# Two half-image stores become one whole-image store, and the load of x is written one stage later

## Chip, cores and metric

The kernel runs on one core of a Trainium2 chip. The metric is the device time of one execution in microseconds (us). Before the change three runs took 1347.35, 1353.44 and 1364.31 us, so the median is 1353.44 us. A comparison of two kernels of this kind can tell about 2% from no change.

## The reference

The input `x` is 32 images of 256 channels by 32 x 32 pixels, in float32. Two layers are applied one after the other, each on a group norm of its input, and each added to its input:

```
x = x + conv3x3_quantised(group_norm(x), weight, bias)      # 256 -> 256 channels, values rounded to fp16's grid
x = x + involution7x7(group_norm(x))                        # 16 groups of 16 channels
```

The convolution rounds its inputs, weights and products to a 5-bit-exponent, 10-bit-mantissa float. The involution computes a 7 x 7 kernel for every pixel and group from the pixel itself:

```
y = relu(w1 @ x * scale + shift)             # 64 channels
w = w2 @ y + b2                              # 16 groups * 49 taps, for each pixel
out[g, c, h, w] = sum over 49 taps of w[g, tap, h, w] * x[g, c, h+i, w+j]
```

## The kernel before

One image is a tile `x` of 128 partitions x 2 halves of channels x 1024 pixels in float32: 8192 B a partition, 1 MB in all. The pool `xpool` has five such tiles, so the tile of image b is used again by image b + 5. An image goes through these steps:

- `load_x` (L106) loads the tile with two DMAs of 512 KB, in runs of 4096 B, from the queue of SyncE (SP).
- `front` does both group norms on ScalarE and VectorE, the 3 x 3 convolution on TensorE (the matmuls of L332), the residual, `w1` (L377) and the transposition of pixels to partitions (L396).
- `weights` (L411) multiplies by `w2`; VectorE evicts the result into `w_sb` (L435).
- `scatter` (L476) writes `w_sb` to a buffer `wd` in DRAM, seven DMAs of 160 KB for each band of 8 image rows (`k` = 0 to 3), in runs of 640 B, from SP's queue. They come in two parts: four DMAs, and three a stage later.
- `load_bands` (L497) reads `wd` back in a skewed form, 16 DMAs a band: two from SP's queue, 14 from GpSimd's (POOL). There are three band buffers, so a band's load waits until the band three places before it has been used.
- `sums` (L522) contracts the bands with the pixels on TensorE, and `add_windows` (L538) adds the result into the image's tile on VectorE.
- `store` (L543) writes a half of the image (512 pixels of every channel, 512 KB in runs of 2048 B) to the output, from SP's queue.

The order of the work is written out by hand. A loop runs over stages n; an image takes 16 stages (`per = 2 * M` with M = 8), and each step has a lag that says at which stage it is written down. Every engine then carries out its own instructions in that order and waits where data is not there. SyncE does nothing but issue DMAs, in order: one that must wait holds up all that stand behind it. In terms of the stage within an image's turn of `sums` (modulo 16), SP's queue holds:

```
stage  3: 4 scatters (k=0), 2 band loads     stage  4: 3 scatters (k=0)
stage  7: 4 scatters (k=1), 2 band loads     stage  8: 3 scatters (k=1)
stage 11: 4 scatters (k=2), 2 band loads     stage 12: store of the first half, 3 scatters (k=2)
stage 13: 4 scatters (k=3)                   stage 14: 3 scatters (k=3)
stage 15: store of the second half, 2 band loads
stage 17: 2 loads of x, for the image five places later, into the tile that was just stored
```

That is 40 DMAs an image. The scatters belong to the next image or the one after it, since `weights` runs 18 stages ahead. SP's DMAs take their completion semaphores from a ring of eight: an SP DMA waits until the one eight places before it has landed. The load of x waits as well until the store of the tile's former image has landed.

The second half's store is written down right after the image's last `add_windows`, which is the last to write the tile. The load's stage comes from `LOAD = -63`: image b is loaded at stage 16 b - 63, which is stage 17 of image b - 5. `front` starts on it at 16 b - 56.

Of the kernel before, what the change touches and what calls it, by code (L numbers as in the profile page):

```python
# [14 lines left out]
B, C, H, W = 32, 256, 32, 32  # L15
N = H * W
NT = 512
# [23 lines left out]
SIDES = 2  # L41
JC = W // SIDES
K = H // TR
M = K * SIDES
# [26 lines left out]
EARLY = CH + 4 + CH * CR  # L71
LATE = K1 * SW + 2 * 2 * SW
FRONT = -56
LOAD = -63
LEAD = 18


# [1 line left out]
def tile_quant_conv_then_involution(  # L79
# [23 lines left out]
    def load_x(b):  # L103
        xt = xpool.tile([P, CH, N], F32, tag="x", name=f"x_{b}")
        for h in range(CH):
            nc.sync.dma_start(xt[:, h], x[b, h * P : (h + 1) * P])  # L106
        return xt
# [85 lines left out]
    def quantize_weights(kh):  # L193

        nc.vector.tensor_scalar(wq[:, kh], staged[kh], F16_MAX, -F16_MAX, ALU.min, ALU.max)
        nc.gpsimd.memset(bands[kh], 0.0)
        if kh == CH - 1:
            nc.gpsimd.memset(w_sb, 0.0)
# [204 lines left out]
    def weights(b, r0):  # L403

        pws = [ps_w.tile([P, 2, 2, SW], F32, tag=f"pw{i}", name=f"pw{i}") for i in range(2)]
        for r in range(2):
            for t in range(T):
                for i in range(2):
                    half = slice(i * CR, (i + 1) * CR)
                    dj = slice(2 * t, min(2 * t + 2, K1))  # L410
                    nc.tensor.matmul(  # L411
                        pws[i][t * TW : (t + 1) * TW, : dj.stop - dj.start, r],
                        y_sb[b % 2][half, (r0 // 2 + r) * W : (r0 // 2 + r + 1) * W],
                        w2_sb[half, dj],
                        start=True,
                        stop=True,
                    )
        for i in range(2):
            for e in range(2):
                p = P if e == 0 else (K1 // 2) * TW  # L420
                for r, rows, d0, d1, at in ring_pieces(b, r0 + 2 * i):
                    evict(pws[i][:p, e, r : r + rows], e, r, rows, d0, d1, at)
# [42 lines left out]
    def scatter(b, k, part):  # L465

        at = (b * H + k * TR) % RING
        for dj in range(part, K1, 2):
            t, e = divmod(dj, 2)
            to = bass.AP(  # L470
                tensor=wd.tensor,
                offset=wd.offset + k * TR * ROW + dj * WPIX + (K1 - 1 - dj) * WB,
                ap=[[WPIX, TW], [ROW, TR], [1, WB]],
            )
            rows = w_sb[t * TW : (t + 1) * TW, e, at : at + TR]
            nc.sync.dma_start(to, rows.rearrange("p s a r v -> p s (a r v)"))  # L476

    def load_bands(b, k):

        band = bands[(b * K + k) % NBAND]  # L480
        side = WINC * WB + PAD
        for i, j in enumerate(ORDER):
            cut = max(0, PAD1 - j)
            n = (K1 - cut) * WB + PAD
            src = bass.AP(
                tensor=wd.tensor,
                offset=wd.offset + k * TR * ROW + (j + PAD1) * WPIX + cut * WB,
                ap=[[ROW - V, TR], [(W - 1 - 2 * j) * WPIX - cut * WB, SIDES], [1, n]],
            )
            to = band[j::JC]  # L490
            to = bass.AP(
                tensor=to.tensor,
                offset=to.offset + (j + cut) * WB,
                ap=[to.ap[0], [side + (JC - 1 - 2 * j - cut) * WB, SIDES], [1, n]],
            )
            queue = nc.sync if j in BY_SYNC else nc.gpsimd
            queue.dma_start(to, src)  # L497
# [10 lines left out]
    def sums(b, m):  # L508

        k, d = divmod(m, SIDES)  # L510
        j0 = 0 if d else PAD1
        band = bands[(b * K + k) % NBAND][:, d]
        px = pixels[(b * K + k) % NPIX][:, d]
        for h in range(CH):
            for v in range(2):
                for g, at, top, f, l in windows(b, m):
                    p = slice(g * KP, (g + 1) * KP)
                    of = band[p, V * g * XR + j0 * WB : V * g * XR + (j0 + WINI) * WB]
                    of = of.rearrange("p (j a r v) -> p j a r v", a=A, r=WIN, v=V)
                    for t in range(T):  # L520
                        a = h * T + t
                        nc.tensor.matmul(  # L522
                            at[t * TW : (t + 1) * TW, h, :, f - top : l - top],
                            px[p, a, v * GC : v * GC + TW],
                            of[:, :, a, f - top : l - top, v],
                            start=(h, v) == (0, 0),
                            stop=(h, v) == (CH - 1, 1),
                        )

    def add_windows(b, m):  # L530

        d = m % SIDES
        to = x_tiles[b].rearrange("p h (r c) -> p h r c", c=W)
        j0 = d * (JC - PAD1)
        for g, at, top, f, l in windows(b, m):
            x_at = to[:, :, f:l, j0 : j0 + WINI]
            of = at.rearrange("p h j r -> p h r j")[:, :, f - top : l - top]
            nc.vector.tensor_tensor(x_at, of, x_at, ALU.add)  # L538

    def store(b, k):  # L540

        cols = slice(k * NT, (k + 1) * NT)
        nc.sync.dma_start(out[b].rearrange("(h p) n -> p h n", p=P)[:, :, cols], x_tiles[b][:, :, cols])  # L543


# [3 lines left out]
    def due(n, lag):  # L549

        b, i = divmod(n - lag, per)
        return (b, i) if 0 <= b < B else (None, None)

    with tc.manual_schedule():
        fronts = {}
        for n in range(FRONT, B * per + 2):
            b, i = due(n, FRONT)
            if i == 0:
                fronts[b] = front(b)
            later = list(fronts)  # L560
            for part in range(2):
                for b in list(later):
                    got = next(fronts[b], fronts)
                    if got is fronts:
                        fronts.pop(b)
                    if got is not LATER:
                        later.remove(b)
            if n in (FRONT + CH, FRONT + CH + 4):
                quantize_weights((n - FRONT - CH) // 4)
            b, i = due(n, 0)  # L570
            if b is not None and i % 2 == 0:
                sums(b, i // 2)
            b, i = due(n, 1)
            if b is not None and i % 2 == 0:
                add_windows(b, i // 2)
                if i // 2 == M - 1:
                    store(b, 1)
                    x_tiles.pop(b)

            b, i = due(n, 2)  # L580
            if b is not None and i == 2 * (M - 1 - SIDES):
                store(b, 0)
            b, i = due(n, -LEAD)
            if b is not None and i % 2 == 0:
                weights(b, i // 2 * WR)

            for part in range(2):
                b, i = due(n, -LEAD + 1 + part)
                if b is not None and i % 2 == 0:
                    for k in range(K):  # L590
                        if i // 2 == min((k + 1) * TR // WR, H // WR - 1):
                            scatter(b, k, part)
            b, i = due(n, LOAD)
            if i == 0 and b > 1:
                x_tiles[b] = load_x(b)

            b, i = due(n, 3 - 4 * NBAND)
            if b is not None and i % 4 == 0:
                load_bands(b, i // 4)
# [38 lines left out]
```

## Time and profile before

| | before |
|---|---|
| median of 3 runs | 1353.44 us |
| the profiled execution | 1344.24 us |
| its span in the profile | 1342.5 us |
| TensorE matmul, busy | 1253.6 us, 93% |
| VectorE, busy | 818.8 us, 61% |
| ScalarE, busy | 733.3 us, 55% |
| GpSimd, busy | 1014.4 us, 76% |
| moved by DMA | 361.85 MB, 270 GB/s on the mean |

Busy time is the time in which an engine has an instruction in work. SyncE has no row of its own: its instructions only issue DMAs. Sixteen DMA engines carry all queues' transfers; q1 is the queue of SP, and q0 that of GpSimd. A packet is one contiguous run of bytes that a DMA engine moves. In a list of waits, a row names the waiting engine and line, then what ended the wait, then the microseconds in total, how often, and the longest.

### The profile page before, as it was taken

What the parts mean: (1) busy time and instruction counts of PE and PEld (TensorE: products, weight loads), DVE (VectorE), ACT (ScalarE), POOL (GpSimd) and SP (SyncE); (2) the same over time, 40 slices, a digit from 0 to 9 for tenths busy, and PEclk for the clock granted to TensorE, in tenths of its full rate; (3) what the DMA queues carried; (4) which work ended last, traced back from release to release, by engine and by line L of the source; (5) the groups of instructions that cost most, each with busy time, mean ns of one, the idle gap of its engine ahead of it and who ended that gap; (6) DMA issues with size and microseconds to landing.
All of it is one profiled execution on the core that took longest, in us unless ns stands there. A gap on an engine that the chain in (4) does not pass through costs nothing.

```text
span 1342.5 us, 65799 instructions
## 1 busy us (share of the span) xinstructions
PE 1253.6 (93%) x27648; PEld 763.7 (57%) x27648; DVE 818.8 (61%) x2539; ACT 733.3 (55%) x1731; POOL 1014.4 (76%) x1818
## 2 busy tenths in 40 slices
PE   5899999999999999999999999999999999999665
PEld 2356566565555655556655556666555566556454
DVE  3466666565666665656665666766666666666442
ACT  5775656455656556556545655655556564553300
POOL 9067878777787778777778787788777877788785
PEclk9999999999999999999999999999999999999987
DMA  6089999999999999999999999999999999999995
GB/s 228 11 237 295 271 293 293 279 266 281 272 286 282 291 285 270 283 263 280 293 282 283 270 288 282 293 297 296 281 288 275 277 284 290 271 281 266 278 274 166
DMA packets 360724, 361.85 MB, mean 270 GB/s; under 512 B 75056, under 2 KB 304752, under 8 KB 359152
## 3 DMA queue, kind: packets, MB, share of 16 engines
q1 hardware_dynamic: 278512, 229.38, 56.8%
q0 software_dynamic: 81920, 128.28, 33.9%
q8 instruction: 220, 3.60, 1.1%
q14 instruction: 72, 0.59, 0.1%
HBM read 176.60 MB, written 180.76 MB: 266 GB/s over the span
## 4 chain that ended last, share of the span: by engine, by line
PE 60%; DMA 23%; POOL 7%; issue 3%; ACT 3%; DVE 2%; SPq 1%; POOLq 0%; DVEq 0%; ACTq 0%
PE pc L332 25%; PE acc L522 19%; DMA band<-wd 17%; PE pw L411 11%; POOL band L497 7%; DMA wd<-w_sb 6%; PE pt L396 3%; PE py L377 3%; ACT junk L214 1%; SPq L476 1%; DVE w_sb L435 1%; DMA x<-in_x 1%; ACT xn L273 0%; SPq L497 0%; ACT xq L273 0%
## 5 line engine op out<-in xcount | busy, mean ns | idle before, releaser
L497 POOL DMA_DIRECT2D band<-wd x1792 | 980.3, 549 | 315.7 <-DMA band<-wd 182.0
L435 DVE TENSOR_TENSOR w_sb<-pw,late_sb 128x224 f32<-128x224 f32 (+7 forms) x1280 | 330.4, 322 | 419.5 <-PE pw L411 419.2
L332 PE MATMUL pc<-xq,wq 128*128 128x496 f16 (+3 forms) x2304 | 535.2, 379 | 20.3 <-ACT xq L273 18.3
L522 PE MATMUL acc<-band,pixels 64*32 64x190 f32 (+1 forms) x16384 | 426.6, 332 | 51.8 <-DMA band<-wd 42.7
L522 PEld LDWEIGHTS acc<-band,pixels 64*32 64x32 f32 x16384 | 304.7, 107 | 159.7 <-issue 81.1
L332 PEld LDWEIGHTS <-wq 128*128 128x128 f16 x2304 | 206.7, 98 | 316.1 <-issue 102.7
L411 PE MATMUL pw<-late_sb,y 64*32 64x224 f32 (+1 forms) x8192 | 288.9, 333 | 10.8 <-issue 9.4
L538 DVE TENSOR_TENSOR x<-acc,x 128x380 f32<-128x380 f32 (+1 forms) x512 | 262.0, 512 | 32.2 <-PE acc L522 23.2
L411 PEld LDWEIGHTS pw<-late_sb,y 64*32 64x32 f32 x8192 | 186.5, 106 | 38.1 <-issue 21.0
L400 ACT COPY pixels<-pt 128x512 f32<-128x512 f32 x128 | 73.7, 576 | 228.6 <-PE pt L396 228.6
L214 ACT ACTIVATE junk<-x 128x512 f16<-128x512 f32 (+1 forms) x192 | 146.4, 763 | 14.7 <-DVE x L348 12.2
L214 ACT ACTIVATE junk<-x,mean 128x1024 f16<-128x1024 f32 x128 | 147.1, 1149 | 4.3
L245 ACT ACTIVATE s<-back,eps 128x2 f32<-128x2 f32 x64 | 18.9, 296 | 178.6 <-DVE back L230 178.6
L346 DVE TENSOR_SCALAR q<-pc 128x512 f16<-128x512 f32 x128 | 87.2, 681 | 17.6 <-PE pc L332 17.6
L273 ACT ACTIVATE xn<-x,off,rstd 128x512 f32<-128x512 f32 x128 | 96.2, 800 | 0.0
L348 DVE SCALAR_TENSOR_TENSOR x<-q,early_sb,x 128x512 f32<-128x512 f16 x128 | 94.2, 736 | 0.3
L396 PEld LDWEIGHTS pt<-ident,xn 128*128 128x128 f32 x512 | 63.9, 142 | 26.3 <-issue 2.5
L396 PE MATMUL pt<-ident,xn 128*128 128x128 f32 x512 | 78.0, 275 | 0.1
L273 ACT ACTIVATE xq<-x,off,rstd 128x1024 f16<-128x1024 f32 x64 | 75.7, 1227 | 0.0
L235 ACT ACTIVATE mean<-back 128x2 f32<-128x2 f32 x64 | 12.6, 196 | 101.4 <-DVE back L230 101.4
L377 PE MATMUL py<-xn,early_sb 128*64 128x512 f32 x256 | 62.2, 606 | 0.9 <-ACT xn L273 0.9
L224 DVE STREAM_TRANSPOSE across<-sums 128x32 f32<-128x32 f32 x128 | 26.3, 205 | 33.6 <-ACT junk L214 32.4
(40 smaller groups left out, 369.3 us busy)
## 6 DMA issues: line engine op xcount, KB each, us to landing
wd<-w_sb SPq DMA_DIRECT2D x896, 160.0 KB
band<-wd POOLq DMA_DIRECT2D x1664, 70.5 KB, 4.6
x<-in_x SPq DMA_DIRECT2D x64, 512.0 KB
out<-x SPq DMA_DIRECT2D x64, 512.0 KB
band<-wd POOLq DMA_DIRECT2D x128, 60.5 KB, 4.6
band<-wd SPq DMA_DIRECT2D x128, 50.5 KB
band<-wd SPq DMA_DIRECT2D x128, 40.5 KB
band<-in_w SPq DMA_DIRECT2D x2, 1152.0 KB
```

The costliest lines, as they stand in the source:

```text
L214: nc.scalar.activation(junk[:, n0:n1], src[:, h, n0:n1], func, bias=bias, accum_out=self.sums[:, i : i + 1])
L273: nc.scalar.activation(dst, src, AF.Identity, bias=self.off[:, one], scale=self.rstd[:, one])
L332: nc.tensor.matmul(pc.rearrange("p (r c) -> p r c", c=W)[:, r0 - nt * RT : r1 - nt * RT, c0:c1], wq[:, kh, k, mh * P : (mh + 1) * P], xq[: ...
L346: nc.vector.tensor_scalar(q, pc, F16_MAX, -F16_MAX, ALU.min, ALU.max)
L348: nc.vector.scalar_tensor_tensor(xt[:, mh, cols], q, bias_sb[:, mh : mh + 1], xt[:, mh, cols], ALU.add, ALU.add)
L377: nc.tensor.matmul(py[i * CR : (i + 1) * CR], w1_sb[:, kh, :], px[:, :, i], start=kh == 0, stop=kh == CH - 1,)
L396: nc.tensor.transpose(pt[:, i, h * P : (h + 1) * P], xn[:, h, (m + i) * P : (m + i + 1) * P], ident)
L411: nc.tensor.matmul(pws[i][t * TW : (t + 1) * TW, : dj.stop - dj.start, r], y_sb[b % 2][half, (r0 // 2 + r) * W : (r0 // 2 + r + 1) * W], w ...
L435: nc.vector.tensor_tensor(to, of[:, :, d0:d1], bias[:, :, d0:d1], ALU.add)
L497: queue.dma_start(to, src)
L522: nc.tensor.matmul(at[t * TW : (t + 1) * TW, h, :, f - top : l - top], px[p, a, v * GC : v * GC + TW], of[:, :, a, f - top : l - top, v], ...
L538: nc.vector.tensor_tensor(x_at, of, x_at, ALU.add)
```

## The change

The store of an image is one DMA at stage 15, 1 MB in runs of 4096 B, for the first 31 images. The last image is stored in halves as before, at stages 12 and 15. The load of x is written down at stage 16 b - 62 instead of 16 b - 63.

```diff
-LOAD = -63
+LOAD = -62
...
-    def store(b, k):
+    def store(b, *halves):
 
-        cols = slice(k * NT, (k + 1) * NT)
+        cols = slice(halves[0] * NT, (halves[-1] + 1) * NT)
         nc.sync.dma_start(out[b].rearrange("(h p) n -> p h n", p=P)[:, :, cols], x_tiles[b][:, :, cols])
...
                 if i // 2 == M - 1:
-                    store(b, 1)
+                    store(b, *([1] if b == B - 1 else range(2)))
                     x_tiles.pop(b)
 
             b, i = due(n, 2)
-            if b is not None and i == 2 * (M - 1 - SIDES):
+            if b == B - 1 and i == 2 * (M - 1 - SIDES):
                 store(b, 0)
```

## The prediction

> **What bounds the kernel now.** I read the page's head and its 40 slices first, then the steady stretch from 165 to 1197 us by itself, then the waits of SP's queue in that stretch, because both edits are in that queue.
>
> ```profile
> PE 1253.6 (93%) x27648; PEld 763.7 (57%) x27648; DVE 818.8 (61%) x2539; ACT 733.3 (55%) x1731; POOL 1014.4 (76%) x1818
> DMA  6089999999999999999999999999999999999995
> ```
>
> The DMA row is 9 from the fifth slice to the last but one, and TensorE is nearly as full. The stretches table sharpens this (columns: length, then each engine's busy time, the granted clock, the DMA engines' busy share, GB/s):
>
> ```profile
> 165.00:1197.00 1032.00, 1003.57 (x22468) 610.87 (x22465) 659.84 (x2059) 594.81 (x1407) 795.15 (x1454) 1.00 0.97 283
> ```
>
> TensorE is busy 1003.57 of 1032 us and the sixteen DMA engines 0.97 of the time. Both are near full. Between the ends of successive images' last `add_windows` lie 39.66 us on the mean (28 images), 37.84 at least, 42.36 at most; the eight shortest average 38.17. The DMA engines' own work is 0.9655 x 39.66 = 38.3 us an image, so neither resource leaves much room. Waits of the same stretch:
>
> ```profile
> POOL band L497 <- DMA band<-wd: 156.5, 195, 2.9
> ...
> POOL band L497 <- DMA wd<-w_sb: 21.3, 22, 3.1
> ...
> PE acc L522 <- DMA band<-wd: 12.7, 10, 2.7
> ```
>
> GpSimd's wait for its own earlier transfers is back-pressure of full engines; its wait for scatters is 0.8 us an image; TensorE waited for a band ten times. The waits of SP's queue:
>
> ```profile
> SPq L476 <- DVE w_sb L435: 79.4, 53, 5.1
> SPq L106 <- DMA out<-x: 72.9, 26, 4.1
> SPq L476 <- DMA wd<-w_sb: 31.8, 50, 2.2
> ...
> SPq L476 <- DMA x<-in_x: 13.5, 18, 1.6
> ```
>
> The second row is the one the change touches: 26 times the load of x stood 2.8 us for the store to land, with all scatters behind it. One such place, in SP's own order:
>
> ```profile
> 649.34 0.94 SPq L543 DMA_DIRECT2D out<-x  x1
> 650.37 1.79 SPq L497 DMA_DIRECT2D band<-wd  x2
> 654.91 0.83 SPq L106 DMA_DIRECT2D x<-in_x  x2
> 656.10 3.05 SPq L476 DMA_DIRECT2D wd<-w_sb  x4
> ```
>
> SP is idle from 652.16 to 654.9; the scatters then follow without a gap, so they were ready and late.
>
> **LOAD.** Between stage 15 (store, two band loads) and stage 19 (the next scatters) SP's queue holds nothing but the two loads. Moving them from stage 17 to 18 moves them past no DMA of SP and none of POOL: both queues keep their order, and what the loads wait for is unchanged. Cost: 0, from both sides. The work that hides any later landing is `front`, which starts six stages on, about 15 us (16 stages in 39.66 us); the loads' packets end 6.65 us after issue (mean of 25 images).
>
> **The first half's store goes** (31 images). SP loses one issue of 0.504 us (median of the 64), 15.6 us in all. It stands in a stretch (8 us before the image's end to 6 us after) in which SP issues without pause: its waits there sum to about 1.5 us an image. So what follows on SP comes earlier: by 0.5 us at least, and by up to 1.9 us if the transfer's own engine time counts too (256 packets x 87 ns / 16 = 1.39 us). Room for that exists: the second store issues 3.3 us after the `add_windows` it needs (mean of 25).
>
> **Packets of 4096 B.** The trace's packet records give, in the steady stretch, 35.6 ns for the 640 B writes (median 32) and 87.1 ns for the 2048 B stores (median 84). A line through the medians is 8.4 ns + 0.0369 ns a byte, hence 160 ns for a 4096 B store; the median of the 4096 B loads is 159. One packet instead of two saves 8.4 ns; 256 pairs / 16 engines x 8.4 = 0.13 us an image, **4.2 us** over 31. The other end is the loads' mean, 213 ns, which would add 39 ns a pair: +0.62 us an image, +19 us. I take the line, because the store rows show no tail (87 against a median of 84), unlike the loads.
>
> [...]
>
> **The store lands later after its issue, from an earlier issue.** Mean of 25 images for the second half's store: first packet 2.19 us after issue, last 3.08 us later, the load 0.57 us after that, the load's first packet 1.11 us on. The new store has the same 16 packets an engine, each longer. Kept at the same share of the engines, 3.08 becomes 3.08 x 160/87 = 5.7 (+2.6 us). At the pace of the x load (32 packets an engine in 5.5 us) it is 2.8 (-0.3). With the earlier issue (-0.5 to -1.9) the load moves by something between **-2.2 and +2.1 us**. I take 0: from the first store's issue to the second's landing the engines are full (0.97 and 1.01 before 653 in the table below), and the same bytes have to pass before the load may go, wherever in that stretch they stand.
>
> The load's place also makes a dip, which does not grow with the store: q1 is empty for 0.57 + 1.11 us whatever was stored.
>
> ```profile
> 645.00:649.00 4.00, 4.00 (x106) 2.63 (x87) 2.61 (x8) 1.66 (x2) 2.16 (x5) 1.00 1.01 286
> 649.00:653.00 4.00, 4.00 (x108) 2.78 (x107) 2.09 (x7) 1.21 (x3) 3.80 (x7) 1.00 0.97 292
> 653.00:656.00 3.00, 3.00 (x98) 2.47 (x102) 2.30 (x8) 1.96 (x4) 2.51 (x5) 1.00 0.93 287
> ```
>
> [...]
>
> What a shift of the load costs: behind it stand the scatters of band 0, and GpSimd's loads of that band wait for those, 0.59 us on the mean. Their last packet lands 2.8 us before TensorE uses the band. In the images with the longest periods GpSimd didn't wait there at all, and over 25 images the load's lateness and the period don't rise together (correlation -0.27). So a shift of a few tenths is absorbed.
>
> **Sum.** LOAD 0, shift 0, packets -4.2: 1344.24 - 4.2 = 1340.0 us for the profiled execution (span 1342.5 and 1.7 around it). The median before stands 0.68% above it; so scaled, **1349 us**. SP's 0.5 us are counted inside the shift.
>
> **Rivals.**
>
> *Slower.* The landing takes the larger figure, SP's stall grows from 2.8 to nearly 5 us, the scatters of band 0 are later by up to 2.1 us, and GpSimd, which has only 0.59 us of wait to lose there, starts the band later. For it: the row of 72.9 us. Against: TensorE's lead of 2.8 us, and the work that is conserved. It decides from 1 us an image on (27 waiting loads, 27 us = 2%). At 1.4 us, two thirds of the bound: +38 - 4 = 1378, scaled **1387**; at all 2.1, +57, 1406.
>
> *Faster.* SP is what lags: everything behind the first store moves up, scatters land before GpSimd asks, and the dip is filled. The dip costs 0.66 us an image (mean shares 0.97, 0.85, 0.75, 0.77 from 7 to 11 us after the image's end), SP's issue 0.5: 27 x 1.16 + 4.2 = 36, 1308, scaled **1317**. For it: SP's unbroken issue. Against: 0.97 of DMA share, and the floor of 38.17 us an image, which allows 40 us at most.
>
> *It does not do what it says.* A 4096 B store costs what the loads cost on the mean: +19, 1363, scaled **1372**, still within 2%.
>
> **How the numbers follow.** Forecast 0.46 (own range 1338 to 1362), costlier packets 0.17, slower 0.21, faster 0.16. About 2% is what a measurement of this kernel can tell from no change; the first two lie within it, 0.63. The range runs from just inside the fast rival to the slow one's first price: 1320 to 1387, leaving out a tenth on each side.
>
> **What will show it.** 4096 B store packets near 160 ns; 8192 fewer q1 packets or slightly less; SP's wait for the store between 2 and 4 us a load; GpSimd's wait for scatters near 21 us in the stretch; the DMA share still 0.97 and the mean period 39.5 us. Wrong if that wait passes 4 us and GpSimd's wait for scatters doubles (slower), or if the period comes near 38.2 (faster).

## The result and the profile after

The changed kernel takes **1368.33 us** (median of 16 runs) where the kernel before took 1355.22 (16 runs): a ratio of **1.0101, 95% interval 1.0079 to 1.0124** (the quotient of the two medians is 1.0097). The loss is small, within 2%, and its interval leaves 1 out. The profiled execution after has a span of 1370.0 us. The one of before, 1344.24 us with a span of 1342.5, is faster than all 16 runs of before (1344.98 to 1364.31), which matters below.

The page of the changed kernel, first TensorE's row and the DMA slices, then the packets and the stretch from 165 to 1197 us:

```profile
PE 1257.5 (92%) x27648; PEld 762.3 (56%) x27648; DVE 825.9 (60%) x2539; ACT 734.0 (54%) x1731; POOL 1012.4 (74%) x1818
...
DMA  6088999999999989999999999999999999999995
...
q1 hardware_dynamic: 270080, 229.38, 55.7%
q0 software_dynamic: 81920, 128.28, 33.0%
```

```profile
165.00:1197.00 1032.00, 990.19 (x22039) 601.97 (x22038) 648.18 (x2025) 580.80 (x1373) 780.63 (x1427) 0.99 0.94 277
```

The packets of q1 are fewer and their bytes the same. But in the same 1032 us TensorE is busy 990.19 us instead of 1003.57, and the DMA engines 0.94 of the time instead of 0.97: both near-full resources have become less full. Most of that is the one fast execution of before, for a second profile of the same instructions (`halves_load62`, below) reads

```profile
165.00:1197.00 1032.00, 992.64 (x22212) 604.69 (x22219) 650.82 (x2022) 585.49 (x1382) 787.49 (x1435) 1.00 0.95 279
```

The waits of SP's queue, and one store with what follows it:

```profile
SPq L106 <- DMA out<-x: 113.3, 26, 5.8
SPq L476 <- DVE w_sb L435: 95.7, 69, 6.1
```

```profile
661.46 0.43 SPq L543 DMA_DIRECT2D out<-x  x1
661.99 2.55 SPq L497 DMA_DIRECT2D band<-wd  x2
668.94 0.83 SPq L106 DMA_DIRECT2D x<-in_x  x2
670.12 2.61 SPq L476 DMA_DIRECT2D wd<-w_sb  x4
```

SP's wait for the store grew from 72.9 to 113.3 us, 1.6 us an image. It looks like the cause. The experiments speak against it. A first hint is in the means over 25 images: the store is now issued 1.43 us after the image's last `add_windows` instead of 3.33, and the load of x goes out at 9.04 us instead of 9.17. SP waits longer because it arrives earlier; the load and the scatters behind it are where they were.

Waits of TensorE and of POOL's queue in the same stretch:

```profile
POOL band L497 <- DMA band<-wd: 175.8, 192, 3.5
...
POOL band L497 <- DMA wd<-w_sb: 25.9, 30, 2.6
...
PE pw L411 <- issue: 19.8, 15, 2.7
...
PE acc L522 <- DMA band<-wd: 9.7, 11, 2.6
PE acc L522 <- issue: 7.6, 8, 1.9
```

GpSimd waits 19 us longer for its own earlier band transfers (156.5 before), TensorE no longer than before for bands (12.7 before), and its stops that the profile can only call issue are 27 us here; on the same two lines they were 11.8 us before (8.2 and 3.6). What these are is told further down.

### The profile page after: what moved, and what is told of

Its sections match the earlier page's. It is cut to its first block, busy times and chain, and to the rows that moved or that the text cites. A ratio compares the mean times of both kernels' runs of the same rounds, so it can differ in the third digit from the quotient of the medians.

```text
span 1370.0 us, 65799 instructions
## 1 busy us (share of the span) xinstructions
PE 1257.5 (92%) x27648; PEld 762.3 (56%) x27648; DVE 825.9 (60%) x2539; ACT 734.0 (54%) x1731; POOL 1012.4 (74%) x1818
## 4 chain that ended last, share of the span: by engine, by line
PE 64%; DMA 19%; POOL 5%; issue 5%; DVE 3%; ACT 2%; SPq 2%; POOLq 0%; DVEq 0%; ACTq 0%
PE pc L332 26%; PE acc L522 20%; DMA band<-wd 14%; PE pw L411 11%; POOL band L497 5%; DMA wd<-w_sb 4%; PE py L377 3%; PE pt L396 3%; SPq L476 1%; ACT junk L214 1%; DVE w_sb L435 1%; DMA x<-in_x 1%; DMA out<-x 1%; DMA band<-in_w 1%; DVE wq L195 1%
## 5 line engine op out<-in xcount | busy, mean ns | idle before, releaser
L332 PE MATMUL pc<-xq,wq 128*128 128x496 f16 (+3 forms) x2304 | 538.5, 380 | 23.7 <-ACT xq L273 20.6
L522 PEld LDWEIGHTS acc<-band,pixels 64*32 64x32 f32 x16384 | 300.9, 107 | 167.1 <-issue 84.0
```

What stands on the lines that cost most here:

```text
L332: nc.tensor.matmul(pc.rearrange("p (r c) -> p r c", c=W)[:, r0 - nt * RT : r1 - nt * RT, c0:c1], wq[:, kh, k, mh * P : (mh + 1) * P], xq[: ...
L522: nc.tensor.matmul(at[t * TW : (t + 1) * TW, h, :, f - top : l - top], px[p, a, v * GC : v * GC + TW], of[:, :, a, f - top : l - top, v], ...
```

## Experiments

Theory A was that the store's merging costs and the move of the load does nothing; B, that the load's move costs, by the start (the first image ended at 133 us in this profile, at 126 before). Within A: D, the price is SP's wait with the scatters behind it and the dip in the DMA share; S, the price is the burst of 1 MB itself on the DMA engines, whoever waits for it. Ratios are always to the kernel before, run beside it on the same chip.

### One part alone

`whole_load63`: the changed kernel with

```diff
-LOAD = -62
+LOAD = -63
```

> The whole-image store alone, with the load of x written down at stage 17 as before. Theory A (the whole store costs, the load's move does nothing): the ratio to before is that of the change, 1.010 (1.007 to 1.013), and SP's wait of the load for the store is near 117 us as in the changed kernel. Theory B (the load's move costs, through the start: the first image ended 7 us later in the changed kernel's profile): the ratio is 1.000 to 1.004.

Measured: 1.0057 (1.0026 to 1.0087).

`halves_load62`: the kernel before with

```diff
-LOAD = -63
+LOAD = -62
```

> The load's move alone, with the two half stores as before. Theory A: the ratio to before is 1.000 within 0.003, since no DMA of SP's queue changes its place. Theory B: 1.005 to 1.012, with the first image's end near 133 us instead of 126.

Measured: 0.9979 (0.9952 to 1.0007). The first images ended at 126.1 and 125.0 us. B falls, and the late start was that one execution's. The traces say more than the times: as far as they tell, every engine and queue of `whole_load63` has the instructions of the changed kernel, and `halves_load62` those of the kernel before, in the same order and with the same shapes and semaphores. The load's move changes only the place in the text. So these two runs are repeats, and they show the noise between measurements: 0.9979 for a kernel against its like, and 1.0057 where the same instructions gave 1.0101. That spread of 0.4% is a little more than the intervals let one expect, and differences of its size between runs made at different times aren't to be read. The store's merging carries the loss.

`two_at_end`: the same bytes at the same place, in 2048 B runs.

```diff
-                    store(b, *([1] if b == B - 1 else range(2)))
+                    for half in [1] if b == B - 1 else range(2):
+                        store(b, half)
```

> The same 1 MB is stored at stage 15, but as two DMAs of 512 KB in 2048 B runs one behind the other. Theory A1 (the 4096 B packets cost: the sixteen engines finish further apart, and the load waits for the last; POOL's queue gets fewer turns): the ratio falls to 0.998 to 1.004. Theory A2 (bringing all bytes together right before the load costs, whatever their run length): 1.008 to 1.014. The dip in the DMA share 8 to 11 us after an image's end is 0.66 us an image by A1 and about 1.0 us by A2.

Measured: 1.0030 (0.9999 to 1.0061). Beside `whole_load63`'s 1.0057, measured with it, this isn't yet a clear difference. The dip in its profile (the DMA engines' missing share, from 7 to 12 us after an image's end) was 1.07 us an image, as A2 said, and the time was A1's: neither holds as put, and the dip is no measure of the loss.

`whole_late`: the changed kernel with the load behind the next scatters.

```diff
-LOAD = -62
+LOAD = -60
```

> The whole store with the load of x written at stage 20, behind the next seven scatters and two band loads instead of ahead of them. Theory A (the wait of the load for the store, with the scatters behind it and the DMA engines' dip, is the price): the wait of SP for the store falls from 117 us to under 20, the dip is filled, and the ratio to before falls to 1.000 or below, 0.985 to 1.000. Theory C (longer packets and POOL's lost turns during the store are the price, and the wait is only beside it): the wait goes and the ratio stays at 1.006 to 1.012. If x then comes too late for its group norm, ScalarE shows waits for the load of x, and the ratio is above 1.012.

Measured: **1.0203 (1.0161 to 1.0246)**. The load no longer waits for a store at all, and the kernel is slower still. ScalarE did wait for x, 15.4 us in all, so this is also a price of loading late. It needs its partner, which follows.

### Is SP's wait the price? Whole and half stores in pairs

`halves_late` is the kernel before with the load at the same late place.

```diff
-LOAD = -63
+LOAD = -60
```

> The kernel before with the load of x at stage 20. Beside whole_late, whose load didn't wait for the store and which took 1.020 of before: theory D says 1.018 to 1.022, equal to it, because neither waits; theory S says 1.008 to 1.013, lower by the burst's 0.8 to 1.0%.

Measured: 1.0129 (1.0081 to 1.0177). With no wait for the store on either side, the whole store is 0.74% above the half stores. That is S's side, though the two intervals overlap, the two were measured at different times, and ScalarE's wait for x differs too (9.8 us here, 15.4 in `whole_late`).

`whole_split` and `halves_split`: the load of x is cut, channel half 0 where it was and half 1 at stage 21; the same edit in both kernels.

```diff
-    def load_x(b):
-        xt = xpool.tile([P, CH, N], F32, tag="x", name=f"x_{b}")
-        for h in range(CH):
+    def load_x(b, halves=range(CH), xt=None):
+        if xt is None:
+            xt = xpool.tile([P, CH, N], F32, tag="x", name=f"x_{b}")
+        for h in halves:
...
             if i == 0 and b > 1:
-                x_tiles[b] = load_x(b)
+                x_tiles[b] = load_x(b, [0])
+            b, i = due(n, -59)
+            if i == 0 and b > 1:
+                load_x(b, [1], x_tiles[b])
```

> The changed kernel, with the load of x in two places: channel half 0 at stage 18 as now, half 1 (512 KB) at stage 21, behind the next seven scatters. SP's wait for the store stays. Theory R (TensorE's own instruction refills, 16 KB each, wait on the same DMA engines behind the x load and the scatters that pile up behind SP's wait, and TensorE stops): the refills that start 12 to 16 us after an image's end wait less than the 3.4 to 4.0 us of the two kernels with whole stores, TensorE's idle time that the profile puts down to issue falls from 26 to 30 us to under 20 between the first image's end and the 28th's, and the ratio to before falls to 0.995 to 1.004. Theory D (SP's wait for the store and the DMA dip are the price): the wait stays near 117 us and the ratio at 1.005 to 1.012.

> The kernel before, with the load of x in the same two places (half 0 at stage 17, half 1 at stage 21). Theory R: below before, 0.990 to 0.999, with the refills' wait 12 to 16 us after an image's end under the 3.6 to 3.8 us of the two kernels with half stores. Theory D: 0.998 to 1.003, as SP's wait for the store is the same.

Measured: whole 1.0097 (1.0062 to 1.0131), halves 0.9977 (0.9947 to 1.0007), so 1.2% between them. TensorE's issue stops were 20.6 us in `whole_split`, and the refills' wait 12 to 16 us after an image's end did fall, to under 3 us; the time didn't follow. Theory R, in the form that the pile-up behind the x load is the price, falls.

`halves_actload` and `whole_actload`: the loads are issued by ScalarE's queue, so that SP has no wait for a store.

```diff
+        queue = nc.sync if b < 5 else nc.scalar
         for h in range(CH):
-            nc.sync.dma_start(xt[:, h], x[b, h * P : (h + 1) * P])
+            queue.dma_start(xt[:, h], x[b, h * P : (h + 1) * P])
```

(with `LOAD = -61` in both.)

> The kernel before, with the loads of x from the sixth image on issued by ScalarE's queue, at stage 19. SP's scatters stand behind no wait for a store. Theory D: SP's wait had a price, so this is below before, 0.980 to 0.995. Theory S: 0.997 to 1.005.

> The changed kernel with the loads of x on ScalarE's queue at stage 19. Theory D: equal to halves_actload within 0.004, as SP waits in neither. Theory S: 0.006 to 0.011 above halves_actload.

Measured: halves **1.0131** (1.0098 to 1.0164), whole **1.0229** (1.0195 to 1.0263). SP's waits in the two, halves first:

```profile
SPq L477 <- DVE w_sb L436: 204.7, 101, 48.1
SPq L477 <- DMA x<-in_x: 143.0, 55, 6.7
```

```profile
SPq L477 <- DVE w_sb L436: 299.7, 132, 48.3
SPq L477 <- DMA x<-in_x: 130.8, 52, 6.1
```

Hardly a wait for a store is left in either (1.8 and 2.9 us in all). SP now waits for the x load itself, nearly alike in both, which may be why both are slower than before; no run shows it. And the whole store still costs 0.98%. D said at most 0.4% between them, S 0.6 to 1.1. **D falls as the main cause.**

`halves_six` and `whole_six`: six tiles for x, so that the load never waits.

```diff
-    xpool = ctx.enter_context(tc.tile_pool(name="xpool", bufs=5))
+    xpool = ctx.enter_context(tc.tile_pool(name="xpool", bufs=6))
...
-NPIX = 6
+NPIX = 4
```

With four buffers, pixels are written over others that are still to be read, so the second layer's sums are taken with wrong pixels; the work and its order are otherwise the same.

> The kernel before with six tiles for x instead of five (paid for by four buffers of pixels instead of six), so that the load of x waits for a store 18 stages back and stands for nothing. Theory D (SP's wait and the DMA dip behind it have a price): 0.975 to 0.995. If only the store's own burst counts: 0.996 to 1.004. If four buffers of pixels are too few, ScalarE waits for sums and both six-tile kernels are slower by the same.

> The changed kernel with six tiles for x and four buffers of pixels. Against halves_six: theory D says no difference within 0.003, since neither load waits and the dip is gone in both. Theory S (the burst of 1 MB itself, in 4096 B packets, holds POOL's band loads and TensorE's refills up for 3 us) says that the 0.8 to 1.0% between whole and half stores stays.

Measured: halves 1.0731 (1.0689 to 1.0774), whole 1.0706 (1.0665 to 1.0747). No difference, as D said, but in kernels where TensorE waits for ScalarE's pixels for long; of the whole store's:

```profile
PE acc L522 <- ACT pixels L400: 110.0, 60, 4.3
```

Here that other wait sets the period, 7% above before, and a price of the burst of 0.8 to 1.0% may be hidden behind it. The pair doesn't decide between D and S.

### What about the burst costs: run length, bytes, or the size of one DMA?

`halves_load2048`: the kernel before with x loaded in 2048 B runs, to see what run length does to the other transfer of this size.

```diff
-        for h in range(CH):
-            nc.sync.dma_start(xt[:, h], x[b, h * P : (h + 1) * P])
+        for k in range(N // NT):
+            cols = slice(k * NT, (k + 1) * NT)
+            nc.sync.dma_start(xt[:, :, cols], x[b].rearrange("(h p) n -> p h n", p=P)[:, :, cols])
```

> The kernel before, with x loaded in two DMAs of 512 KB in 2048 B runs in place of 4096 B. The same bytes, at the same place. If the run length is what makes refills and POOL's packets wait: the refills' wait 12 to 16 us after an image's end falls below 3.2 us, and the ratio is 0.992 to 0.999. If it is the bytes in the queue: no change of that wait, ratio 0.998 to 1.006.

Measured: 1.0027 (0.9996 to 1.0057); the refills' wait was 3.7 us, unchanged. Run length makes no difference here.

`whole_channels`, and the same kernel again as `channels_again`: the store in 4096 B runs, as two DMAs.

```diff
+        if len(halves) == 1:
+            nc.sync.dma_start(out[b].rearrange("(h p) n -> p h n", p=P)[:, :, cols], x_tiles[b][:, :, cols])
+        else:
+            for h in range(CH):
+                nc.sync.dma_start(out[b, h * P : (h + 1) * P], x_tiles[b][:, h])
```

> The image's store at stage 15 as two DMAs of 512 KB, one for each half of the channels, in 4096 B runs. Beside two_at_end, whose two DMAs have 2048 B runs and which took 1.003: if the run length is what costs, 1.007 to 1.012 as with the one transfer; if what counts is one DMA of 1 MB against two of 512 KB, 1.001 to 1.005.

> Two DMAs of 512 KB in 4096 B runs at stage 15, once more. If the size of the single DMA is the price: 1.002 to 1.006, as two_at_end and two_again with 2048 B runs (1.003 and 1.004). If the run length is: 1.008 to 1.012.

Measured: 1.0048 (1.0014 to 1.0081) and 1.0026 (0.9992 to 1.0059).

`whole_again` and `two_again`: the changed kernel and `two_at_end` once more, side by side.

> The changed kernel once more, beside two_again. 1.006 to 1.012 of before by every theory; its profile adds a second one to that of the first.

> Two DMAs of 512 KB in 2048 B runs at stage 15, once more. If moving the bytes together is the whole price: within 0.003 of whole_again. If run length or the size of one DMA is part of it: 0.004 to 0.007 below whole_again.

Measured: whole **1.0101** (1.0067 to 1.0136), two **1.0039** (1.0015 to 1.0062). The first measurement of the change is repeated, to the fourth digit by luck, and measured together, two DMAs lie below one by 0.6%.

`whole_quarters`: four DMAs of 256 KB in 4096 B runs, in place of the two of `whole_channels`.

```diff
             for h in range(CH):
-                nc.sync.dma_start(out[b, h * P : (h + 1) * P], x_tiles[b][:, h])
+                for p in (0, P // 2):
+                    c = h * P + p
+                    nc.sync.dma_start(out[b, c : c + P // 2], x_tiles[b][p : p + P // 2, h])
```

> The image's store at stage 15 as four DMAs of 256 KB (64 partitions of one channel half each), in 4096 B runs. If the size of the single DMA is the price: 1.001 to 1.005. If the run length is: 1.008 to 1.012, as with the one transfer. Two more issues of SP, 1 us an image, stand before the load of x in either case.

Measured: 1.0058 (1.0030 to 1.0087), a little above what the size of the single DMA promised; its issues took SP 4.05 us an image, and the load of x went out at 11.6 us instead of 9.0, so another price is mixed in.

So two DMAs at the same place cost 0.3 to 0.5% in either run length (two of the four intervals reach 1), and one DMA about 0.9% (1.0101, 1.0057 and 1.0101 for the same instructions). **The run length isn't the price.** Moving the bytes together is a part, and making one DMA of them seems to be another: of the two side-by-side pairs one shows it clearly (1.0101 against 1.0039), the other hardly (1.0057 against 1.0030).

One DMA fewer also shifts the ring of eight (in the traces of before and after, every one of SP's 1287 and 1256 DMAs has the completion semaphore of the one eight places before it): 39 of SP's DMAs an image instead of 40 share it, so each waits for another one than before. That did not cost SP time: its waits for earlier DMAs other than the store sum to 56.8 us in the stretch after, 64.7 before.

`no_store`: the changed kernel without the stores of the first 31 images, which it leaves out.

```diff
-                    store(b, *([1] if b == B - 1 else range(2)))
+                    if b == B - 1:
+                        store(b, 1)
```

> The changed kernel with the stores of the first 31 images left out; the last image is stored. This prices the stores as a whole. SP's wait for the store is gone and 31 MB of 362 are not moved (2.6 us of engine time an image). Theory D and theory R both: the dip is gone, issue stalls under 12 us, the period of an image near TensorE's floor of 37.9 to 38.3 us, ratio 0.955 to 0.975. If the ratio is over 0.985, TensorE and not the DMA traffic sets the period, and both theories fall.

Measured: 0.9864 (0.9818 to 0.9911). All that stores cost in the kernel before is 1.4%; the expected 2.5 to 4.5% was wrong. The line put on record was 0.985: above it TensorE and not the DMA traffic sets the period, and D and S are accounts of a loss at its edge, not of the bound. The ratio is above, its interval not wholly. The whole stores cost 2.4% for the same bytes (1.0101 against 0.9864). In the trace the period of an image is 39.1 us with no store at all, where the kernel before has 39.65 to 40.2 (its own and `halves_load62`'s profile): TensorE's matmuls alone fill 38.3 us of it.

### Where the burst is felt

While a store's packets drain, the other queues get little: q0 has 12 to 24% of the engines in the three drains below, 33.0% over the whole run of the changed kernel. Here are the queues' shares of the sixteen engines in one image's drain, taken as the time from the first twentieth of its packets to nine tenths of them: the kernel before (691.3 to 693.1 us), the changed kernel (704.1 to 706.8) and `channels_again` (732.0 to 734.9).

```profile
q1 hardware_dynamic: 331, 0.54, 82.2%
q0 software_dynamic: 83, 0.14, 24.0%
```

```profile
q1 hardware_dynamic: 280, 0.94, 92.7%
q0 software_dynamic: 69, 0.13, 12.3%
```

```profile
q1 hardware_dynamic: 288, 0.94, 82.0%
q0 software_dynamic: 133, 0.22, 21.1%
```

These three are near their means. Over 23 images, GpSimd's queue q0 had 0.22 of the engines while a half store drained (two profiles), **0.10 to 0.12** with one DMA of 1 MB (three profiles, over a longer drain), 0.17 to 0.19 with two DMAs (four profiles, both run lengths) and 0.30 with four. Taken from the first packet to the last, the shares lie closer: 0.36 to 0.37, 0.28 to 0.29, 0.30 to 0.32 and 0.35. From 3 to 7 us after an image's end GpSimd's share was 0.31 to 0.34 in the kernels with half stores (0.29 with six tiles), 0.30 with the 2048 B loads, 0.24 to 0.26 with two DMAs, and 0.20 to 0.25 with one whole store. GpSimd's wait for its own earlier transfers was 6.0 to 7.3 us an image with half stores and 6.5 to 8.0 with whole ones (5.6 and 6.0 with six tiles). Between partners of the split, late and ScalarE pairs it rose by 0.7 to 1.0 us, but from `halves_load62` to `whole_load63` only by 0.1. That the crowding comes with the single DMA is shown by the shares. That it makes the lost time is only a reading: no experiment removes it alone, and four DMAs, with the largest share left to GpSimd's queue, still cost 0.6%.

Which wait of TensorE carries the time is not the same everywhere. In the pair with ScalarE's queue it is the wait for bands, halves first, from 165 to 1197 us:

```profile
PE acc L523 <- DMA band<-wd: 18.4, 11, 2.7
```

```profile
PE acc L523 <- DMA band<-wd: 30.3, 22, 2.9
```

In the others the bands differ by 0.2 us an image at most, in either direction, and the issue stops tend to rise: 0.46, 0.95, 0.67 and 0.98 us an image with half stores (before, `halves_load62`, `halves_split`, `halves_late`), 1.09, 1.02, 0.93, 0.75 and 1.39 with whole ones (after, `whole_again`, `whole_load63`, `whole_split`, `whole_late`). One profile each, with ranges that overlap. This stays open. So does why one DMA crowds the others more than two of the same bytes.

## Why the prediction was wrong, step by step

- **The time**: 1368.33 us lies in the range, which its width explains, and the chances put most on no change beyond 2%; but the forecast had the sign wrong: -4 us where +13 came.
- **LOAD costs nothing**: right, and for the reason given: no queue's order changes. 0.9979 (0.9952 to 1.0007) alone.
- **The load's shift, "I take 0"**: right. Issue earlier by 1.9 us, the last packet 1.64 us later after it (6.91 us instead of 5.27), the load 0.1 us earlier.
- **The failing step**: the sum gave the burst no price of its own, because the load stood where it stood. "The same bytes have to pass before the load may go" holds for SP's queue: the load went out at 9.04 us, 9.17 before. How they pass is another matter: GpSimd's queue's share in the drain fell from 0.22 to about 0.11, the same bytes in two DMAs cost 0.3 to 0.5% and in one about 0.9%. What the burst takes from the other queues stands neither in the sum nor in the rivals. Longer packets aren't its ground: with two DMAs the share (0.17 to 0.19) and the time (1.0030 and 1.0039 in 2048 B runs, 1.0048 and 1.0026 in 4096 B) are alike. By which wait the burst reaches TensorE stays open.
- **Packets, -4.2 us**: mis-sized, and by 3 us a small part of the miss. The 4096 B store packets have the median of the line, 159 ns, but a mean of 172.6 against 2 x 87.1: 0.03 us an image, under 1 us in all. The argument that stores have no tail came from short ones. Going from 2 to 4 KB brought no gain here, in the store (the four times just given) or, undone, in the load (1.0027).
- **The dip doesn't grow**: unclear. From 7 to 12 us after an image's end it was 0.72 us an image in the profile of before, 0.96 in `halves_load62`, 0.94 to 1.06 with whole stores. The engines do finish further apart: from the time nine tenths of the packets are through to the last it takes 1.48 us instead of 0.90.
- **The slower rival** had the right side and the wrong mechanism: SP's wait grew, to 4.4 us a load, and GpSimd's wait for scatters only from 21.3 to 25.9 us. SP's wait in itself has no visible price in the pairs.
- **The rival of costlier packets** came nearest with its number, 1372 us, by luck: it needed packets of 213 ns, and they took 172.6.
- **The faster rival's floor**: with all 31 stores gone the time falls by 1.4% only, so moving them about would hardly have brought its 36 us.
- **One profile as a base**: the profiled execution of before was among the fastest. Its issue stops, 12.8 us from the first image's end to the 28th's, were half of those in `halves_load62` (25.9), the same instructions in the same order. Differences of 1% can't be read from one profile of each side.

## To carry to other kernels

The 1 MB store was not priced by when its own waiter went on (9.04 us against 9.17): look at what share the other queues keep while a transfer drains (here 0.10 to 0.12 where it was 0.22), above all a queue that feeds the bound engine. With the DMA engines 0.95 to 0.97 busy (the two profiles of before's instructions), one 1 MB store cost 0.6 to 1.0% more than two of 512 KB apart, and two DMAs together 0.3 to 0.5% more, in 2048 B runs as in 4096 B. A wait that grows in the profile, as SP's from 72.9 to 113.3 us, may only be the same moment reached earlier. An edit that changes no queue's order is a repeat, and its spread (0.4% here) is the noise to read other differences by. To test a suspected wait, remove it on both sides of the change and see whether the difference goes.

## What the runs showed of the hardware

TensorE stops for its own instructions. On every one of the stops put down to issue over 0.2 us, before (19 from the first image's end to the 28th's) and after (25), the instruction at which it went on stands at the same place in a block of 256 (number 193 or 194 of TensorE's trace, modulo 256), and each ended 1.2 to 1.7 us after one of 220 packets of 16,384 B on queue q8 had landed. The row of that queue before:

```profile
q8 instruction: 220, 3.60, 1.1%
```

Before, a packet started 2.3 us on the mean after TensorE had entered the block ahead of it, but 3.4 to 4.2 us when that fell 12 to 16 us after an image's end, while the x load was in flight (in the kernels with the load at its old place), and took 1.1 us; with the load at stage 20 the peak moved to 20 to 24 us (3.6 to 3.7). A block lasted 5.6 us there in the median, and 63% of the blocks less than 6.3. So a refill that waits for 4 us, with 1.1 us for the packet and 1.2 us or more behind it, 6.3 us together, comes too late for many blocks and TensorE stops: an estimate from these numbers. Most refills are hidden (186 fall into that stretch, before as after, and 19 and 25 stops). But those that aren't make 13 to 38 us of TensorE's idle time in the kernels with five tiles for x, the most in `whole_late`.
